# When the places of a token list are written out: list scatters paced behind an expert's products

## The chip, the cores and the metric

The kernel runs on one core of a Trainium2 chip. The metric is the device time of one execution in microseconds. The profile is of one further execution, with a record of every instruction and of the transfers.

## The reference

The input is x, 4 batches of 1,024 tokens of 256 numbers, all in float32. There are two layers.

The first is cross attention. The tokens, normalised, are the queries; 77 context vectors per batch give keys and values; there are 16 heads. The result is added to x.

The second is a mixture of experts. Each token, normalised, is sent to 2 of 9 experts by a router, and what the two give is added to it, weighted. What matters here is this part:

```python
logits = jnp.einsum('bsh,he->bse', x, Wr)
probs = jax.nn.softmax(logits, axis=-1)
topk_w, topk_idx = jax.lax.top_k(probs, TOP_K)
topk_w = topk_w / jnp.sum(topk_w, axis=-1, keepdims=True)
...
gate = jax.nn.silu(jnp.einsum('th,ehi->tei', xf, Wg))
hidden = gate * jnp.einsum('th,ehi->tei', xf, Wu)
out = jnp.einsum('tei,eih,te->th', hidden, Wd, cw)
```

An expert has two matrices of 256 x 704 (Wg, Wu) and one of 704 x 256 (Wd). The kernel computes an expert only for the tokens that chose it, so it has to make a list of tokens for each expert first.

## The kernel before

**Groups and their lists.** The 4,096 tokens are worked on in 8 groups of 512 (g = 0 to 7), each as 4 tiles of 128. The attention stage runs over the 32 tiles. For each tile TensorE makes scores (L273), ScalarE exponentials (L288), VectorE divides and turns the weights (an, anT). The turned weights go to memory and come back in another order (a_d, then aT, both on SP's queue), and TensorE multiplies them by the values (L349). Behind a group's last tile comes its routing: `choices(g)` finds the two experts of each token, `ranks(g)` counts with two small products the places in the experts' lists, and `places(g)` turns these into addresses (the tile r_pli). A list entry is a token's number and its weight (r_entry). The lists are one array in the chip's memory, list_d.

**Scatters.** `scatter()` sends one indirect transfer from GpSimd's queue (L990). It writes 128 entries of 8 bytes to 128 places of list_d. A group has 2 x 4 = 8 of them, 64 in all. `places` puts them into a queue in the program, `pending`, and for all groups but one also calls `scatter()` at once, so that they stand in GpSimd's queue right behind that point. The exception is g = NG - 3 = 5, the sixth group: its eight are left in `pending` and taken out later in `hidden_pair`, with a wait on a VectorE product (argument `behind`).

**Blocks.** The experts' work is cut into blocks: pairs (2 x 128 tokens of one expert, `hidden_pair`), ones (128 tokens, `hidden_one`), and flexible ones. Blocks 0 to 5 (EARLY = 6) are pairs that are filled from the first four groups alone (G_EARLY = 4), so that they can start before the last groups are routed. Block 0 runs together with the end of the attention stage. Each block j needs, in this order:

- the token numbers: `tokens(j)`, a gather from list_d to ids (GpSimd, L1234). For j = 0 and for j = 6 it waits until all scatters sent so far have landed;
- the tokens: `inputs(j)`, two gathers of 128 rows from y_d to yin (GpSimd, L1234, one for a block of 128), which need the ids;
- the tokens turned: for early blocks by TensorE (`turn(j)`, L1277) and ScalarE (xT); for later blocks by VectorE (`turning(j)`, L1264);
- the weights, on SP's queue (wgu and wd);
- the products: for a pair and each f from 0 to 5, up to four products of 128 x 256 (pg, L1291), a silu on ScalarE (sl, L1297) and a product on VectorE (hid, L1298);
- the second matrix: `down(j)` (L1371), scaled on VectorE to co (L1374);
- the output: `adding(j)`, indirect transfers with add from GpSimd (L1406).

**The order around the change.** The order on each engine is written out in the program; there is no planner. For block j the loop at L1605 does this: `fetch()` sends what is due ahead (the gathers of the tokens of block j + 2, the token numbers of block j + 4, the weights of block j + 2), then the products of block j, then the turn of block j + 1, then `down(j - 1)` and `adding(j - 1)`. Token numbers of block 6 and later are due only when the tables for the late blocks exist. In between, `pump()` is called behind each f. It runs pieces of the routing of the last two groups and of the late blocks' tables, up to 12 VectorE operations at a time. The routing of group 6 ends with its places in block 1, that of group 7 with its places in block 2. In block 1 the line behind the product, with `len(pending)`, sends all that is left of group 5; the eight of group 6 are sent in block 1 too, and those of group 7 in block 2, at once by `places`.

GpSimd's queue is in order: a gather or an output stands behind every scatter that was put ahead of it. The tiles yin, of which there are three, are used in turn by the blocks; so are three tiles each of r_entry and r_pli by the groups.

Of the kernel before, what the change touches and what calls it, by code (L numbers as in the profile page):

```python
# [21 lines left out]
def kernel(  # L22
# [25 lines left out]
    E, _, FF = wg.shape  # L48
# [5 lines left out]
    NG = TOK // TB  # L54
# [33 lines left out]
    G_EARLY = NG - 4  # L88
    EARLY = 6
# [38 lines left out]
    def mm_tile(name):  # L128
        return ps_mm.tile([P, TB], F32, tag="mm", name=name)
# [715 lines left out]
    def after(i, others, reason):  # L845
        for other in others:
            tc.add_manual_dep(
                i.ins, other.ins.name,
                mybir.DependencyInfo(mybir.DependencyClass.Sync, mybir.DependencyReason.DATA),
                reason=reason,  # L850
            )
# [7 lines left out]
    def small(g, name, shape=(P, NS), dt=F32, **kw):  # L859
        return pools["rpool"].tile(list(shape), dt, tag=f"r_{name}", name=f"r_{name}{g}", **kw)  # L860
# [104 lines left out]
    def places(g):  # L965

        v = nc.vector
        o, pp, entries = (routed[g][k] for k in ("o", "pp", "entries"))
        at = small(g, "at", wide)
        yield v.tensor_tensor(  # L970
            at, pp[:, : NS * E].rearrange("p (s e) -> p s e", s=NS), base, ALU.add
        )
        for k in range(2):
            yield v.tensor_tensor(o[k], o[k], at, ALU.mult)
            place, place_i = small(g, f"pl{k}"), small(g, f"pli{k}", (P, NS), I32, bufs=3)
            yield v.tensor_reduce(place, o[k], AX.X, ALU.add)
            yield v.tensor_copy(place_i, place)  # L977
            for s in range(NS):
                pending.append((place_i, entries[k], s))
                if g != NG - 3:  # L980
                    scatter()

    pending = []

    def scatter(behind=None):

        if not pending:
            return
        place_i, entry, s = pending.pop(0)
        i = nc.gpsimd.indirect_dma_start(  # L990
            out=list_d[:, :],
            out_offset=bass.IndirectOffsetOnAxis(ap=place_i[:, s : s + 1], axis=0),
            in_=entry.bitcast(I32)[:, s, :], in_offset=None,
            bounds_check=E * LP - 1, oob_is_err=False,
        )
        if behind is not None:
            after(i, [behind], "the lists' places go out one by one")

        for other in sent:
            tc.declare_no_dep(i.ins, other.ins, reason="other places of the lists")  # L1000
        sent.append(i)
# [230 lines left out]
    def gather(dst, src, offsets, bound=None):  # L1232
        kw = {} if bound is None else dict(bounds_check=bound - 1, oob_is_err=False)
        return nc.gpsimd.indirect_dma_start(  # L1234
            out=dst, out_offset=None, in_=src,
            in_offset=bass.IndirectOffsetOnAxis(ap=offsets, axis=0), **kw,
        )

    def tokens(j):

        nh, i, kind = blocks[j]
        got = gather(
            ids[j].rearrange("p h t -> p (h t)"), lists[nh], tabs[kind][1][:, i : i + 1]
        )
        if j in (0, EARLY):
            after(got, sent, "all places of the lists")
# [37 lines left out]
    def hidden_pair(j, also={}, upcoming=iter(())):  # L1284

        (w,), xT, hid = wgus.pop(j), xTs.pop(j), hids[j % 2]
        for f in range(NF + 1):
            pg = mm_tile(f"pg{j}_{f}").rearrange("p (g t) -> p g t", g=2)
            for g, at in enumerate((f * P, UP[f]) if f < NF else (f * P,)):
                for c in range(C):  # L1290
                    nc.tensor.matmul(  # L1291
                        pg[:, g, :], w[:, c, at : at + P], xT[:, c, :],
                        start=(c == 0), stop=(c == C - 1),
                    )
            sl = pools["spool"].tile([P, TS], F32, tag="sl", name=f"sl{j}_{f}")
            if f < NF:
                nc.scalar.activation(sl, pg[:, 0, :], AF.Silu)  # L1297
                made = nc.vector.tensor_tensor(hid[:, f, :], pg[:, 1, :], sl, ALU.mult)  # L1298
                for _ in range(0 if not j and f < 4 else 2 if not j else len(pending)):
                    scatter(made)  # L1300
            else:
                nc.scalar.activation(sl[64:128, :], pg[0:64, 0, :], AF.Silu)
                nc.vector.tensor_tensor(
                    hid[64:128, NF, :], pg[64:128, 0, :], sl[64:128, :], ALU.mult
                )
            pump()
            if f > 1:
                advance(upcoming, 4)
            for fn in also.get(f, ()):
                fn()  # L1310
# [109 lines left out]
    def pump():  # L1420

        if held[0]:
            held[0] -= 1
            return
        for _ in range(STEP if rest else 0):
            got = next(rest[0], None)
            if got is None:
                rest.pop(0)
                if not rest:
                    fetch()  # L1430
                return
            if got is PRODUCT:
                held[0] = HOLD
                return
# [3 lines left out]
    def fetch(in_parts=False):  # L1438

        end = NBLK if late_ready() else EARLY  # L1440
        for name, fn, lead in (
            ("weights", weights, LEAD), ("weights_upper", weights_upper, LEAD + 1),
            ("inputs", inputs, LEAD), ("tokens", tokens, LEAD + 2),
        ):
            if name == "inputs":

                while ahead["tokens"] < min(now[0] + LEAD + 1, end):
                    tokens(ahead["tokens"])
                    ahead["tokens"] += 1
            while ahead[name] < min(now[0] + lead + 1, end):  # L1450
                fn(ahead[name], in_parts) if name == "weights" else fn(ahead[name])
                ahead[name] += 1
# [8 lines left out]
    def advance(what, n=None):  # L1461

        for _ in range(n) if n is not None else iter(int, 1):
            if next(what, None) is None:
                return True
        return False
# [11 lines left out]
    def listed(g):  # L1478
        yield PRODUCT
        ranks(g)  # L1480
        yield from places(g)
# [4 lines left out]
    for i in range(N_SUB + 1):  # L1486
        g, s = divmod(i, NS)
# [57 lines left out]
        if gr >= 0 and sr == 1:  # L1545
            if g + 2 < NG:
                query_variance(g + 2)
            if q >= 0:
                advance(residual(q))
                root(q)  # L1550
            if g + 2 < NG:
                query_root(g + 2)
            nc.scalar.activation(junk, eps_t, AF.Exp)
            if q > 0:
                advance(places(q - 1))
# [49 lines left out]
    for j in range(LAST):  # L1605
# [9 lines left out]
        if j == RARE_AT - 1:  # L1615
            tokens(NBLK)
            inputs(NBLK)
# [5 lines left out]
        if blocks[j][0] == 2:  # L1623
            hidden_pair(j, {} if j else in_first, upcoming)
        else:
            hidden_one(j, upcoming)
# [22 lines left out]
    assert not rare  # L1649

    hidden_pair(LAST, {1: [lambda: down(LAST - 1), lambda: adding(*rounds_of(LAST - 1)[0])]})
    down(LAST)
    adding(*rounds_of(LAST)[0])
# [33 lines left out]
```

## Time and profile before

| | |
|---|---|
| median of three runs | 885.0 us (884.68 to 886.63) |
| the profiled execution | 887.22 us |
| its span, first to last instruction | 885.2 us |
| granted TensorE clock | 0.996 |
| TensorE busy | 98% |
| VectorE busy | 67% |
| ScalarE busy | 40% |
| GpSimd busy | 35% |
| list scatters, L990 | 64, of 1,028 ns in the mean, from 163.8 to 422.1 us |
| token gathers, L1234 (yin) | 67, of 1,060 ns in the mean |
| output transfers, L1406 (out_dram from co, ids) | 63, of 1,601 ns in the mean |

The lines of a timeline read so: start in us from the span's start, duration in us, engine, line of the kernel, operation, what it writes <- what it reads, how often; in brackets the idle time of the engine before it and what ended that time. PE is TensorE, DVE VectorE, ACT ScalarE, POOL GpSimd. A POOL row of DMA_INDIRECT is the time in which GpSimd writes the transfer's descriptors; the transfer itself lands later. In the list of waits, the numbers are us in total, how often, and the longest in us. "DMA yin<-y_d,ids" means that the engine waited for this transfer to land. The windows of TensorE's work in the stretch that is spoken of:

| us | work of TensorE |
|---|---|
| up to 352.5 | attention, tile by tile (L273, L349) |
| 352.5 to 371.6 | block 0's products, with the last attention tiles |
| 371.6 to 387.5 | block 1, then `down(0)` |
| 387.5 to 403.2 | block 2, then `down(1)` |
| 403.2 to 420.6 | block 3, then `down(2)` |
| 420.6 to 437.1 | block 4, then `down(3)` |
| 437.1 to 452.2 | block 5, then `down(4)` |

### The profile page before, as it was taken

The numbers are of one execution on the slowest core, as the hardware profiler recorded it, in microseconds if no ns is written. First come the engines' busy times: TensorE is split into PE (matmuls) and PEld (weight loads), VectorE is DVE, ScalarE is ACT, GpSimd is POOL, SyncE is SP. The second block draws the span as 40 slices with busy tenths as digits, with TensorE's granted clock in tenths as the row PEclk, the third lists the DMA queues.
The fourth block names the chain that finished last, engine by engine and source line by source line (L and its number), as shares of the span: only waits on it lengthen the run. The fifth ranks groups of instructions, "written<-read, shape, count | busy, mean of one in ns | idle before, by whom it ended". The sixth has DMA issues, their size and how long they took to land. (4 is left out here: it accounts for less than half of the span.)

```text
span 885.2 us, 13820 instructions
## 1 busy us (share of the span) xinstructions
PE 863.1 (98%) x3864; PEld 676.0 (76%) x3864; DVE 590.8 (67%) x1806; ACT 356.4 (40%) x1500; POOL 313.0 (35%) x325
## 2 busy tenths in 40 slices
PE   7999999999999999999999999999999999999996
PEld 6645787787878778987887777777777777778885
DVE  4857688998989988456445666666666666664641
ACT  3668787978879686241111111111111111111110
POOL 3000000404314350147665435435435444454332
PEclk9999999999999999999999999999999999999999
DMA  6117556667676696978788889769779777779722
GB/s 226 50 56 216 147 169 198 167 210 184 173 203 171 179 243 210 307 239 188 172 241 238 233 260 290 229 213 330 217 223 308 227 224 217 219 230 322 211 24 24
DMA packets 132956, 181.20 MB, mean 205 GB/s; under 512 B 26951, under 2 KB 98127, under 8 KB 132752
## 3 DMA queue, kind: packets, MB, share of 16 engines
q1 hardware_dynamic: 115322, 162.90, 60.2%
q0 software_dynamic: 17344, 17.29, 10.3%
q8 instruction: 31, 0.51, 0.2%
q14 instruction: 45, 0.37, 0.1%
q10 hardware_dynamic: 214, 0.13, 0.0%
HBM read 141.54 MB, written 40.41 MB: 206 GB/s over the span
## 5 line engine op out<-in xcount | busy, mean ns | idle before, releaser
L1291 PE MATMUL pg<-xT,wgu 128*128 128x256 f32 x1144 | 252.7, 379 | 1.6 <-DVEq L1640 1.5
L1291 PEld LDWEIGHTS pg<-xT,wgu 128*128 128x128 f32 x1144 | 215.7, 190 | 31.0 <-issue 1.9
L288 ACT ACTIVATE ex<-psc,mx 128x77 f32<-128x77 f32 x512 | 158.8, 331 | 59.1 <-DVE mx L277 58.9
L1371 PE MATMUL po<-wd,hid 128*128 128x256 f32 (+1 forms) x804 | 180.8, 380 | 0.0
L1371 PEld LDWEIGHTS po<-wd,hid 128*128 128x128 f32 (+1 forms) x804 | 149.2, 187 | 28.0 <-issue 3.7
L990 POOL DMA_INDIRECT list_d<-r_entry,r_pli x64 | 65.8, 1028 | 262.6 <-DVE r_pli L977 136.5
L349 PE MATMUL po<-u,aT 128*128 128x265 f32 x640 | 155.5, 398 | 1.2 <-DMA aT<-a_d 1.2
L1264 DVE STREAM_TRANSPOSE xT<-yin 32x128 f32<-32x128 f32 (+1 forms) x544 | 148.3, 273 | 11.4 <-DMA yin<-y_d,ids 3.2
L1406 POOL DMA_INDIRECT out_dram<-co,ids x63 | 100.8, 1601 | 152.0 <-DVE co L1374 127.9
L349 PEld LDWEIGHTS po<-u,aT 128*128 128x128 f32 x640 | 148.6, 312 | 1.4 <-issue 1.4
L273 PE MATMUL psc<-g,zT 128*128 128x462 f32 (+1 forms) x384 | 140.9, 513 | 1.6 <-ACT zT L262 1.5
L1297 ACT ACTIVATE sl<-pg 128x256 f32<-128x256 f32 x130 | 49.8, 384 | 226.6 <-PE pg L1291 203.0
L1298 DVE TENSOR_TENSOR hid<-pg,sl 128x256 f32<-128x256 f32 x130 | 55.0, 424 | 126.2 <-ACT sl L1297 125.5
L273 PEld LDWEIGHTS psc<-g,zT 128*128 128x128 f32 x384 | 72.1, 190 | 59.0 <-issue 45.8
L288 ACT ACTIVATION_READ_ACCUMULATOR ex<-psc,mx 128x1 f32 x512 | 108.2, 211 | 0.0
L329 DVE STREAM_TRANSPOSE anT<-an 128x1280 f32<-128x1280 f32 x32 | 79.6, 2487 | 2.4 <-DMA a_d<-anT 2.3
L1234 POOL DMA_INDIRECT yin<-y_d,ids x67 | 71.0, 1060 | 24.7 <-issue 18.9
L277 DVE TENSOR_REDUCE mx<-psc 128x6 f32<-128x462 f32 (+1 forms) x96 | 53.4, 556 | 23.2 <-PE psc L273 23.2
L1374 DVE TENSOR_SCALAR co<-po,ids 128x256 f32<-128x256 f32 x67 | 32.2, 483 | 52.6 <-PE po L1371 51.0
L310 DVE TENSOR_TENSOR an<-ex,rs 128x1024 f32<-128x1024 f32 x32 | 39.2, 1225 | 1.1
L1359 ACT COPY hid<-ph 128x384 f32<-128x384 f32 x15 | 7.2, 479 | 78.4 <-PE ph L1354 78.4
L1335 ACT ACTIVATE hs<-psg 128x512 f32<-128x512 f32 x15 | 9.0, 597 | 65.3 <-PE psg L1331 65.3
(311 smaller groups left out, 762.8 us busy)
## 6 DMA issues: line engine op xcount, KB each, us to landing
wgu<-in_L_ffn_Wg_dram SPq DMA_DIRECT2D x41, 704.0 KB
wd<-in_L_ffn_Wd_dram SPq DMA_DIRECT2D x41, 640.0 KB
wgu<-in_L_ffn_Wu_dram SPq DMA_DIRECT2D x41, 512.0 KB
a_d<-anT SPq DMA_DIRECT2D x32, 640.0 KB
aT<-a_d SPq DMA_DIRECT2D x128, 160.0 KB
wgu<-in_L_ffn_Wu_dram SPq DMA_DIRECT2D x41, 128.0 KB
x<-in_x_dram SPq DMA_DIRECT2D x8, 512.0 KB
out_dram<-x SPq DMA_DIRECT2D x8, 512.0 KB
```

The source lines that it names most:

```text
L273: nc.tensor.matmul(psc[:, :w], zT[:, c, :], g_sb[i // NS // GPB][:, c, h * J : h * J + w], start=(c == 0), stop=(c == C - 1),)
L277: nc.vector.tensor_reduce(nmx[i][:, h : h + n], psc[:, : n * J].rearrange("p (h j) -> p h j", h=n), AX.X, ALU.max, negate=True,)
L288: nc.scalar.activation(exs[i][:, h + q, :], pscs[k][:, q * J : (q + 1) * J], AF.Exp, bias=nmx[i][:, h + q : h + q + 1], accum_out=sms[i][: ...
L329: nc.vector.transpose(turned.rearrange("p q t k -> p q k t"), an_of[0].rearrange("p (k q t) -> p q k t", q=NQ, t=Q))
L349: nc.tensor.matmul(po[:, :DE], aT[:, :, n], u_sb[b][:, n, :], start=(n == 0), stop=(n == KC - 1))
L990: i = nc.gpsimd.indirect_dma_start(out=list_d[:, :], out_offset=bass.IndirectOffsetOnAxis(ap=place_i[:, s : s + 1], axis=0), in_=entry.bit ...
L1234: return nc.gpsimd.indirect_dma_start(out=dst, out_offset=None, in_=src, in_offset=bass.IndirectOffsetOnAxis(ap=offsets, axis=0), **kw,)
L1264: yield nc.vector.transpose(xT[q : q + Q].rearrange("p c (h t) -> p h c t", t=P)[:, :nh, :, a : a + Q], of(yins, j)[a : a + Q].rearrange(" ...
L1291: nc.tensor.matmul(pg[:, g, :], w[:, c, at : at + P], xT[:, c, :], start=(c == 0), stop=(c == C - 1),)
L1298: made = nc.vector.tensor_tensor(hid[:, f, :], pg[:, 1, :], sl, ALU.mult)
L1371: nc.tensor.matmul(po[rows, :D], hid[:, f, at], d[:, f, :], start=(f == 0), stop=(f == NF))
L1406: i = nc.gpsimd.indirect_dma_start(out=out_r, out_offset=bass.IndirectOffsetOnAxis(ap=rows_of(j, h, rows), axis=0), in_=cos[j][:, h, :], i ...
```

## The change

Three places of the program are edited.

1. `places`: the scatters of groups 0 to 3 are sent at once, as before. Those of groups 4, 5, 6 and 7 are now all left in `pending`.
2. `hidden_pair`: behind the VectorE product of each f from 0 to 4, scatters are taken from `pending`, each with a wait on that product. In block 0 it is none behind f = 0 and up to four behind each of f = 1 to 4; in block 1 none; in later blocks up to two behind each product.
3. `tokens`: ahead of the token numbers of block 6, what is left in `pending` is sent.

With this the queue of GpSimd holds, in block 0, the 16 scatters of groups 4 and 5; in block 2, the eight of group 6 and two of group 7; in block 3, behind f = 0, 1 and 2, the other six. None is left for block 4 or for the third edit.

```diff
             for s in range(NS):
                 pending.append((place_i, entries[k], s))
-                if g != NG - 3:
+                if g < G_EARLY:
                     scatter()
...
         nh, i, kind = blocks[j]
+        while j == EARLY and pending:
+            scatter()
         got = gather(
             ids[j].rearrange("p h t -> p (h t)"), lists[nh], tabs[kind][1][:, i : i + 1]
         )
...
                 made = nc.vector.tensor_tensor(hid[:, f, :], pg[:, 1, :], sl, ALU.mult)
-                for _ in range(0 if not j and f < 4 else 2 if not j else len(pending)):
+                for _ in range((0, 4)[f > 0] if not j else 2 if j > 1 else 0):
                     scatter(made)
```

`pending`, `scatter` and `after`, which the wait is made with, are as they were.

## The prediction

> **What bounds the kernel now.** I read first the page's busy times and the list of TensorE's waits, then TensorE's timeline at each of its stops, last GpSimd's timeline, since GpSimd's queue is what the edit rearranges.
>
> ```profile
> PE 863.1 (98%) x3864; PEld 676.0 (76%) x3864; DVE 590.8 (67%) x1806; ACT 356.4 (40%) x1500; POOL 313.0 (35%) x325
> ...
> PE px L1277 <- DMA yin<-y_d,ids: 2.8, 3, 1.8
> PE po L349 <- DMA aT<-a_d: 1.2, 1, 1.2
> ```
>
> TensorE is the bound: 98% busy at a granted clock of 0.996. So the edit can only win time where TensorE stands still. Of its stops between 300 and 450 us just these two kinds are listed, 4.0 us together; past 450 us the next gap is one of 1.5 us at 812 us, at a branch that the edit doesn't touch. Here are the four stops in the timeline:
>
> ```profile
> 333.33 4.93 PE L349 MATMUL po<-u,aT 128*128 128x265 f32 x20 [1.18 <-DMA aT<-a_d]
> ...
> 414.85 0.74 PE L1277 MATMUL px<-ident,yin 128*128 128x128 f32 x4 [1.77 <-DMA yin<-y_d,ids]
> ...
> 430.66 0.30 PE L1277 MATMUL px<-ident,yin 128*128 128x128 f32 x1 [0.39 <-DMA yin<-y_d,ids]
> 431.56 0.55 PE L1277 MATMUL px<-ident,yin 128*128 128x128 f32 x3 [0.60 <-DMA yin<-y_d,ids]
> ```
>
> The stops at 414.85 and 430.66 are the turns of the tokens of blocks 4 and 5. Why these come late stands in GpSimd's timeline:
>
> ```profile
> 371.66 1.07 POOL L990 DMA_INDIRECT list_d<-r_entry,r_pli  x1 [45.08 <-DVE hid L1298]
> ...
> 386.80 1.02 POOL L990 DMA_INDIRECT list_d<-r_entry,r_pli  x1 [5.45 <-DVE r_both L934]
> ...
> 403.51 0.98 POOL L990 DMA_INDIRECT list_d<-r_entry,r_pli  x1 [0.30 <-issue]
> ...
> 405.95 1.62 POOL L1406 DMA_INDIRECT out_dram<-co,ids  x1 [0.80 <-DMA wgu<-in_L_ffn_Wu_dram]
> ...
> 410.30 1.08 POOL L1234 DMA_INDIRECT yin<-y_d,ids  x1 [0.30 <-DVE pair_sum L1025]
> ...
> 427.13 1.08 POOL L1234 DMA_INDIRECT yin<-y_d,ids  x1 [0.30 <-issue]
> ...
> 434.19 1.02 POOL L1234 DMA_INDIRECT ids<-list_d,pair_ai  x1 [0.30 <-issue]
> ...
> 439.76 1.04 POOL L1234 DMA_INDIRECT yin<-y_d,ids  x1 [4.56 <-PE pg L1291]
> ```
>
> GpSimd is idle for 45 us, then sends 14 scatters in one run from 386.80 (1.285 us from start to start). Block 0's output, ready on VectorE from 389.25 (co, L1374), waits behind them to 405.95, and block 4's token gather to 410.30. It lands at 414.7, TensorE wanted it at 413.1. Eight more scatters at 413 to 423 hold block 5's gather to 427.13 in the same way; it is wanted at 429.9.
>
> **The change, part by part.** The counts stay: 64 scatters, the same gathers and outputs, no instruction more on TensorE, VectorE or ScalarE. What moves is the order in GpSimd's queue, and each position follows from the program text.
>
> (1) Group 4's eight scatters leave 310.46 to 320.5. The gather for block 2 that stood behind them (321.64 and 323.60) can run at about 303.5, once its token numbers have landed (303.1 in the trace's DMA records). This matters at 333.33: the weights aT of that product land at 332.4 after 5.4 us of transfer (512 packets of 1,280 bytes), where the next two aT take 3.5 and 3.4 us. The gather's 64 packets of 4,096 bytes, 269 ns each, lie at 325.7 to 331.1, inside it: 64 x 0.269 / 16 engines = 1.08 us. By bytes, 0.26 MB at about 330 GB/s, it is 0.8. From landing to the product took 0.9 us, and TensorE was ready at 332.15. So of the 1.18 I take 0.9 away; the ends are 0 (other transfers fill the place) and 1.18. At 303.5 the gather meets the aT landing at 307.5, used at 313.8: cover of over 5 us, so nothing there. The scatters themselves are 16 packets of 64 bytes at 14 to 19 ns and cost the transfers nothing, here and in block 0, where the DMA engines are full (share 0.89 to 1.05 from 352 to 387).
>
> (2) Block 0 now issues 16 scatters, four behind each of the products f=1 to 4 (361.2, 363.6, 364.6, 371.0 in the old trace). The first waits where GpSimd was idle anyway, with only group 6's token numbers and later scatters close behind. 16 x 1.285 = 20.6 from 360.6, plus 0.7 for the copies between: GpSimd is through at about 382. Block 3's gather comes next, 382 instead of 374.34, landing by about 389 (6.6 us as before); it is wanted at 397.6, so the cover is 8.6 less the 0.9 gained, 7.7. The token numbers of block 5 wait for the last scatter to land, about 387, and hold up block 0's output, which isn't ready until 388.3.
>
> (3) Block 1 issues none, so that output goes at about 389.5 and block 4's gather at 393.5 instead of 410.30. It lands near 400, wanted at 412: the 1.77 us go, with 12 us to spare.
>
> (4) Block 2 issues ten (about 396 to 409), then block 1's output to 412.7 and block 5's gather at 413 instead of 427.13, landing by 420. TensorE, now 2.7 us ahead, wants it at 427: the 0.99 us go, with 7 to spare.
>
> (5) The last six go in block 3 behind f=0 to 2. VectorE is late there with the late blocks' tables (its f=2 product ran at 411.18, 2 us behind ScalarE), so they run from 416 to 423.3. Block 2's output follows to 427. Block 6's token numbers need all scatters landed: 422 + 6.6 to 8.0 (landings at that load) = 430, instead of 434.19. They land 4.8 later, and block 6's gather goes at 435.6, its data in by 439.5. Before it was 439.76, with the last packet at 443.6 and TensorE at 446.62. TensorE will be there at 442.9: cover 3.4, before 3.0. This is the tightest place. From there GpSimd is about 4 to 5 us earlier than before and TensorE 3.7, so nothing later loses cover.
>
> The waits on products hold GpSimd alone. Behind its tile reuse nothing is late: VectorE's entries of group 7 reuse group 4's tile, whose scatters have landed by about 376 and are needed landed at 388.
>
> Here the Trainium skill speaks against the change. "SBUF — State Buffer", in "SBUF: two separate sides", says that GpSimd can't write descriptors while a VectorE copy holds the port pair that they share, and that a GpSimd transfer of 620 ns took 3,100 beside one. Pacing scatters behind VectorE's work invites that. The row: 64 scatters of 972/980/1644 ns (least, median, most), and the run of 14 beside VectorE's products and group 7's small operations has none over 1.02 us. By the row the pacing costs nothing. By the page, 16 x 2.5 = 40 us more in block 0 would bring block 3's gather to 422, and TensorE would stop for 40 - 7.7 = 32 us at 397: a sum of 885.2 - 3.7 + 32 = 914. I take the row, 881.5.
>
> A second rule sizes the chain of (5). "DMA: Bandwidth & Descriptors", "Anatomy of one DMA — SWDGE (gpsimd) path", gives about 2 us for a small transfer. The trace's scatters land after 2.8/4.7/8.1. By the page the cover at block 6 would be 11 us instead of 3.4; I keep the row.
>
> Sum: 0.9 + 1.77 + 0.99 = 3.66. The profiled execution has a span of 885.2 and 887.22 in all; its span should become 881.5. The median of the three timed runs, 885.0, lies within 0.2 of that span, and I take the same 3.7 off: 881.3. Each us that TensorE starts earlier should reach the end, as the tail (8.2 us of outputs behind the last product) is unchanged.
>
> **The rivals.** Partly: the stop at 333 stays, because the output and weight transfers queued there fill the gap, or half of block 5's stays. Then 2.76 or 2.3 are saved: 882.2 to 882.7. For it: DMA share 0.91 from 310 to 333.5 without any help from GpSimd. Against: the 5.4 beside 3.5 us. Chance 0.15.
>
> Given back: the landings in (5) take 8 us three times over instead of 8, 4.8 and 4, so block 6's gather is in at about 446.5, and 3.6 is lost there again: about 884.9, no change. For it: old landings up to 8.9 at 447. Against: scatters and block 2's output are over by 427, and the DMA share of 0.81 from 420 to 437 is 0.60 behind that. Chance 0.10.
>
> Slower: the port lock. Its place is the scatters of blocks 0 and 2, beside VectorE's small copies. What a scatter takes over 1.285 us from start to start counts 16-fold ahead of block 3's gather. With the cover of 7.7 block 3 is late from 1.77 us on, and from 2.0 us on more is lost than the 3.7 gained. At 2.2 the time is about 888, at the page's price 914. For it: four of the earlier scatters took 1.50 to 1.64. Against: no more than one in a run of eight did, and the others took about 0.98. Chance 0.06.
>
> That the order doesn't change can't be: the positions are fixed in the program.
>
> **How the numbers follow.** All three gains 0.69, at 881.3, own range 880.5 to 882.0; partly 0.15; given back 0.10; slower 0.06. A measurement of this kernel tells 0.2% (1.8 us) from no change: the three runs spread over 1.95. Faster is the first two less 0.02, for a mixture in which only one stop goes: 0.82. Those 0.02 and most of the third make same 0.11; the rest, with the fourth, makes slower 0.07. The range leaves out the lower tail of the first case and everything slower than a nearly full give-back: 880.2 to 883.8.
>
> **What would show it.** Right: no stop of TensorE before L1279 (the turn's new line) at blocks 4 and 5; the stop before L349 at 332 under 0.4 us; GpSimd's first wait on a product at 361 instead of 371; block 0's output at about 390. Wrong: a stop of TensorE at block 3 (397) or at block 6 (443), scatters over 1.6 us in block 0, or aT later than 332.4.

## The result, and the profile after

The changed kernel took 890.8 us (median of 13 runs, 888.43 to 894.43) against 887.87 us for the kernel before beside it (13 runs, 884.68 to 889.48): a ratio of 1.004, interval 1.0026 to 1.0055. It is slower, by 0.4%; 881.3 with a range up to 883.8 was forecast. Ratios and intervals, here and below, are taken over the fast runs and aren't quotients of the medians shown. The profiled execution took 891.61 us, span 889.6, clock 0.995; the span of before was 885.2.

The page and TensorE's list of waits from 300 to 460 us, changed kernel (us in total, times, longest):

```profile
PE 864.9 (97%) x3864; PEld 676.9 (76%) x3864; DVE 591.2 (66%) x1806; ACT 356.4 (40%) x1500; POOL 312.1 (35%) x325
...
PE px L1279 <- DMA yin<-y_d,ids: 5.9, 3, 2.8
PE psc L273 <- ACT zT L262: 0.4, 1, 0.4
```

The stop before L349 is gone from the list, a wait of 0.42 us for ScalarE at 300 us is new, and the waits for token gathers have grown from 2.8 to 5.9 us. TensorE's timeline shows where:

```profile
332.39 4.86 PE L349 MATMUL po<-u,aT 128*128 128x265 f32 x20
...
412.21 0.60 PE L1279 MATMUL px<-ident,yin 128*128 128x128 f32 x4
...
428.67 0.64 PE L1279 MATMUL px<-ident,yin 128*128 128x128 f32 x4 [1.18 <-DMA yin<-y_d,ids]
429.14 5.35 PE L1373 MATMUL po<-wd,hid 128*128 128x256 f32 x24
...
445.82 0.30 PE L1279 MATMUL px<-ident,yin 128*128 128x128 f32 x1 [1.84 <-DMA yin<-y_d,ids]
448.96 0.90 PE L1279 MATMUL px<-ident,yin 128*128 128x128 f32 x3 [2.83 <-DMA yin<-y_d,ids]
449.65 7.13 PE L1373 MATMUL po<-wd,hid 128*128 128x256 f32 x24
```

The stops at 333 and at block 4's turn are gone, block 5's is still there (1.18), and block 6's turn, where before had none, stands for 1.84 + 2.83 = 4.67 us. Behind it the same 24 products of `down` take 7.13 us instead of 5.35. TensorE's windows there say why (length, busy time and count, granted clock, DMA share, GB/s):

```profile
core 0: us, PE busy (x), PEclk, DMA share, GB/s
...
444.00:446.44 2.44, 0.30 (x1) 1.00 0.60 162
446.44:453.27 6.83, 4.31 (x12) 0.50 0.91 235
453.27:466.00 12.73, 12.73 (x61) 1.00 0.73 208
```

The clock is halved for 6.83 us. TensorE worked 4.31 us of these, so that costs about 2.15 (half of the work, an estimate). Without its stops and this the changed kernel would have 889.6 - 1.18 - 4.67 - 2.15 = 881.6; the kernel before without its four stops has 885.2 - 3.94 = 881.3. So stops and clock account for the difference within 0.3 us. Of the forecast gain of 3.66 us, 2.95 is there (the stop at 333 and block 4's turn); block 5's 0.99 isn't, and what is lost on top is at block 6's turn.

GpSimd's timeline tells why these gathers are late:

```profile
360.89 1.03 POOL L990 DMA_INDIRECT list_d<-r_entry,r_pli  x1 [53.56 <-DVE r_top L931]
...
381.37 0.98 POOL L990 DMA_INDIRECT list_d<-r_entry,r_pli  x1 [0.31 <-issue]
382.66 1.05 POOL L1234 DMA_INDIRECT yin<-y_d,ids  x1 [0.31 <-issue]
...
394.67 0.98 POOL L1234 DMA_INDIRECT ids<-list_d,early_ai  x1 [9.63 <-DMA list_d<-r_entry,r_pli]
...
397.13 1.65 POOL L1408 DMA_INDIRECT out_dram<-co,ids  x1 [0.81 <-DMA wgu<-in_L_ffn_Wu_dram]
...
400.94 1.08 POOL L1234 DMA_INDIRECT yin<-y_d,ids  x1 [0.30 <-issue]
...
420.60 1.07 POOL L1234 DMA_INDIRECT yin<-y_d,ids  x1 [0.30 <-issue]
...
429.79 0.98 POOL L990 DMA_INDIRECT list_d<-r_entry,r_pli  x1 [0.30 <-DMA list_d<-r_entry,r_pli]
...
438.79 1.02 POOL L1234 DMA_INDIRECT ids<-list_d,pair_ai  x1 [4.26 <-DMA list_d<-r_entry,r_pli]
442.83 1.04 POOL L1234 DMA_INDIRECT yin<-y_d,ids  x1 [3.03 <-issue]
```

The 16 scatters of block 0 go as forecast, 360.89 to 381.37. Then the read of block 5's token numbers (394.67) waits 9.63 us, until the last of them has landed at 393.92: 12.55 us after its issue. From there GpSimd has no pause until 434.5. Block 0's output goes at 397.13 instead of 389.5, and everything behind it is 7 to 9 us later than forecast: block 4's gather, block 5's, the last scatter, block 6's token numbers, block 6's gather.

### The profile page after: what moved, and what is told of

Its sections match the earlier page's. It is cut to its first block, busy times and chain, and to the rows that moved or that the text cites. A ratio compares the mean times of both kernels' runs of the same rounds, so it can differ in the third digit from the quotient of the medians.

```text
span 889.6 us, 13823 instructions
## 1 busy us (share of the span) xinstructions
PE 864.9 (97%) x3864; PEld 676.9 (76%) x3864; DVE 591.2 (66%) x1806; ACT 356.4 (40%) x1500; POOL 312.1 (35%) x325
## 5 line engine op out<-in xcount | busy, mean ns | idle before, releaser
L1293 PE MATMUL pg<-xT,wgu 128*128 128x256 f32 x1144 | 252.7, 379 | 1.6 <-DVEq L1642 1.5
L1293 PEld LDWEIGHTS pg<-xT,wgu 128*128 128x128 f32 x1144 | 215.7, 190 | 31.0 <-issue 1.9
L1373 PE MATMUL po<-wd,hid 128*128 128x256 f32 (+1 forms) x804 | 182.6, 382 | 0.0
L1373 PEld LDWEIGHTS po<-wd,hid 128*128 128x128 f32 (+1 forms) x804 | 150.5, 189 | 28.5 <-issue 3.7
L349 PE MATMUL po<-u,aT 128*128 128x265 f32 x640 | 155.4, 398 | 0.0
L349 PEld LDWEIGHTS po<-u,aT 128*128 128x128 f32 x640 | 148.7, 312 | 0.1
```

Source lines behind the costliest of these rows:

```text
L349: nc.tensor.matmul(po[:, :DE], aT[:, :, n], u_sb[b][:, n, :], start=(n == 0), stop=(n == KC - 1))
L1293: nc.tensor.matmul(pg[:, g, :], w[:, c, at : at + P], xT[:, c, :], start=(c == 0), stop=(c == C - 1),)
L1373: nc.tensor.matmul(po[rows, :D], hid[:, f, at], d[:, f, :], start=(f == 0), stop=(f == NF))
```

## The experiments

Two theories at first. The *landing theory*: the wait for the landings of block 0's scatters, in front of block 5's token numbers, makes GpSimd late. The *pace theory*: the waits behind products in blocks 2 and 3 spread the scatters too far, whatever happens in block 0. There were five batches, each on one chip, each with the kernel before beside it:

| batch | before, us | what ran |
|---|---|---|
| 1 | 899.88 (67 runs) | e1 to e4 |
| 2 | 885.85 (62) | e5 to e8 |
| 3 | 887.35 (25) | e9 to e12 |
| 4 | 888.19 (23) | e13 to e16 |
| 5 | 887.26 (17) | e17, e18 |

**Batch 1: four parts of the change.** e1 reads block 5's token numbers ahead of block 0's scatters:

```diff
-            ("inputs", inputs, LEAD), ("tokens", tokens, LEAD + 2),
+            ("inputs", inputs, LEAD), ("tokens", tokens, LEAD + 2 + (now[0] == 0)),
```

e2 sends group 4's scatters at once again (`if g < G_EARLY + 1`), so that block 0 has eight; e3 those of groups 6 and 7 (`if g < G_EARLY or g > NG - 3`). e4 asks for block 3's weights one block later, so that they aren't transferred under block 0's scatters:

```diff
-            ("weights", weights, LEAD), ("weights_upper", weights_upper, LEAD + 1),
+            ("weights", weights, LEAD - (now[0] == 1)), ("weights_upper", weights_upper, LEAD + 1),
```

> The changed kernel with one gather moved: the token numbers of block 5 are read before block 0's sixteen scatters, so that GpSimd no longer waits, between blocks 0 and 1, until the last of these has landed (10.7 us from the gather at 384.0 to 394.67 in the changed kernel). Landing theory (the scatters land late while the DMA engines are full, 12.6 us for the last instead of the 6.6 that I reckoned with, and this one wait hands that to everything behind it): block 0's output goes at about 389 instead of 397.1, blocks 5 and 6 get their tokens 7 us earlier, the stops of 1.18 and 4.67 us are gone, and with them the halved clock behind the second: span about 882, ratio to the kernel before 0.995 to 0.998. Pace theory (two scatters behind each product reach into block 3 whatever comes before, and block 6's list is complete too late): the stop at block 6 stays over 3 us, ratio 1.002 to 1.005.

> The changed kernel with group 4's eight scatters sent at once, as in the kernel before; blocks 0, 2 and 3 keep the fixed pace. Block 0 then sends eight scatters, not sixteen. Landing theory: the last of them is sent at about 372 and landed by 380, the token numbers of block 5 go at about 380, block 0's output at 389; no stop at blocks 5 and 6, but the stop of about 1.2 us at 333 (weights of the attention behind block 2's gather) is back: span about 883, ratio 0.996 to 0.999. Pace theory: as the changed kernel, a stop over 3 us at block 6, ratio 1.002 to 1.005.

> The other half alone: groups 4 and 5 go behind block 0's products as in the changed kernel, groups 6 and 7 are sent at once in blocks 1 and 2, as in the kernel before. Landing theory: the token numbers of block 5 go at 394.7 as in the changed kernel, then group 6's eight scatters, block 0's output at 406, block 4's tokens asked for at 410 and landed by 416, wanted at 412: a stop of 3 to 5 us at block 4 with a halved clock behind it; none at block 6, whose list is complete earlier. Span 888 to 891, ratio 1.002 to 1.006. Pace theory: the late pace was the cause and is gone, so this one is as fast as the kernel before or faster, 0.996 to 1.000.

> The changed kernel, with the order of GpSimd's queue untouched, but the weights of block 3 (2.1 MB) asked for one block later, so that these transfers are not among those that fill the DMA engines from 371 to 387. Landing theory: the last scatter of block 0 lands within about 8 us instead of 12.6, block 5's token numbers go at about 389 instead of 394.7, and the stops at blocks 5 and 6 shrink from 5.9 us together to under 1.5: span 882 to 885, ratio 0.996 to 1.000. If the DMA load has nothing to do with the late landings, nothing changes: ratio 1.002 to 1.005, last landing still over 11 us.

Measured: 900.6 (ratio 1.000, 0.9978 to 1.0022), 896.63 (0.9969, 0.9951 to 0.9988), 896.93 (0.9968, 0.995 to 0.9986), 900.24 (1.0009, 0.9987 to 1.0031). By the ratios e2 lies in the landing theory's range, e3 in the pace theory's, and e1 and e4 in neither. This chip ran the kernels some 11 to 18 us longer, the one before by 12 to 14, and in these traces TensorE stood before the products of `hidden_pair` and `down` (L1293, L1373), as in none of the others, and nowhere for a gather. So I take no verdict on the theories from them; why this chip differs is open. One reading remains: with the weights moved away (e4), block 5's token numbers went at 384.43 after a wait of 0.58 us, in e3, with the same scatters ahead, at 390.87 after 5.73.

**Batch 2: both kernels unedited, and the two edits again.**

> The kernel before, unedited, for its trace on the chip of this batch. Both theories: ratio 1.000 within the noise; stops before the turns of blocks 4 and 5 and before the attention product at 333, as in its first trace. If the stops lie elsewhere (at products that wait for ScalarE or VectorE, as in the four traces of the last batch), this chip shows a disturbance of its own, and ratios from it say little about either theory.

> The changed kernel, unedited, beside it. Both theories: ratio 1.002 to 1.006, stops at blocks 5 and 6, the token numbers of block 5 held back behind the last scatter of block 0.

> The changed kernel with the token numbers of block 5 read before block 0's scatters, again, now beside traces of both kernels on the same chip. Landing theory: faster than the changed kernel by 0.4 to 0.9%, no stop at blocks 5 and 6. Pace theory: as the changed kernel.

> The changed kernel with group 4 sent at once, again. Landing theory: faster than the changed kernel by 0.3 to 0.8%, a stop of about 1.2 us at 333, none at blocks 5 and 6. Pace theory: as the changed kernel.

| | median us (range) | ratio to before, interval | token numbers of 5 | block 0's output | block 6's second gather | stops at block 6 |
|---|---|---|---|---|---|---|
| e5, before | 884.28 (883.3 to 886.03) | 0.9983, 0.9969 to 0.9998 | 379.83 | 404.83 | 438.90 | none |
| e6, changed | 884.43 (880.73 to 889.79) | 0.9988, 0.9974 to 1.0003 | 391.35 | 393.81 | 440.61 | 0.88 |
| e7, numbers first | 882.55 (880.38 to 884.38) | 0.9966, 0.9954 to 0.9977 | early | 389.34 | 433.94 | none |
| e8, group 4 at once | 882.17 (880.15 to 885.24) | 0.9962, 0.9951 to 0.9973 | 378.96 | 387.82 | 432.76 | none |

On this chip the changed kernel equals the one before, which neither theory had given. e5 and its partner are one program, and yet its interval leaves out 1: differences of about 0.2% don't separate two kernels here. e7 and e8 are 0.2 and 0.3% under e6, less than the landing theory gave. But they keep the pace of blocks 2 and 3 and have no stop between 300 and 800 us but one of 0.19 (e8, before L349): the pace theory falls. The landing theory stands so far.

**Batch 3: the weights again, and the same edit in the kernel before.** e9 is the changed kernel, e10 is e4's edit, e11 is the kernel *before* with e1's edit, e12 has the edits of e7 and e8 together.

> The changed kernel unedited, as the partner of the other three. Landing theory: its time hangs on when the last scatter of block 0 lands. If block 5's token numbers go by 391.5, as on the quiet chip, it stands within 0.15% of the kernel before; if they go at 394 or later, as in the first profile, TensorE stops at block 6's turn for over 2 us and the ratio is 1.002 to 1.006. Pace theory: a stop behind the products of blocks 2 and 3 in every run, 0.3% to 0.5% above before.

> The weights of block 3 are asked for one block later, so that they are no longer transferred under block 0's scatters; the scatters are as in the changed kernel. If the transfers of weights are what holds the landings up: the last scatter lands within 5 us, block 5's token numbers go by 386, no stop at the turns of blocks 4 to 6, and the time is that of the two edits that took the wait away (ratio about 0.9965), unless block 3's weights now come late at 396 (a stop there of up to 2 us, ratio up to 0.999). If the number of scatters in flight holds them up: the token numbers still go at 390 or later and the time is that of the changed kernel beside it.

> The kernel before with the one edit that helped the changed kernel: block 5's token numbers are read one block earlier. Landing theory: before has two scatters ahead of these token numbers in block 0, and its stops at the turns of blocks 4 and 5 come from the 14 scatters in one run, which stay; so within 0.15% of before. If that edit helps by itself, whatever the pace: ratio 0.9965, as with the changed kernel.

> The changed kernel with both edits: the fifth group's scatters go at once, and block 5's token numbers are read one block earlier. Landing theory: each edit alone already takes every stop between 300 and 800 us away, so together they bring no more: ratio to before 0.996 to 0.997, no stop. If the two act on different losses: 0.994.

Measured: e9 890.89 (880.82 to 894.5; 1.0008, 0.9979 to 1.0037; the quotient of the medians would be 1.004), e10 882.33 (0.9935, 0.9912 to 0.9958), e11 883.09 (0.994, 0.9917 to 0.9963), e12 884.01 (0.9958, 0.9942 to 0.9975). e12 is as expected, no more than either edit alone, but for a stop of 0.97 us at 333. e10 has no stop, but the last scatter still took 7.57 us to land and the token numbers went at 389.43, not by 386: its gain can't come from that wait alone. And e11 contradicts the theory as I had put it: the edit helps before as much. Its GpSimd timeline:

```profile
375.44 1.04 POOL L1234 DMA_INDIRECT yin<-y_d,ids  x1 [0.30 <-issue]
376.79 1.02 POOL L990 DMA_INDIRECT list_d<-r_entry,r_pli  x1 [0.31 <-DVE mv_f L879]
...
396.43 1.62 POOL L1406 DMA_INDIRECT out_dram<-co,ids  x1 [0.80 <-DVE hid L1298]
```

The run of 14 scatters starts at 376.79, not at 386.80. What held it in before was the read of block 5's token numbers from the list. (The program text asks for a wait for all scatters at blocks 0 and 6 alone; in the traces this read waits for those ahead of it too.) It waited for two scatters to land and went at 380.38; it landed at 386.04, and the next scatter, which writes the list that it reads, went 0.76 us later (in e5: 384.88, and 0.76 later). The profile had put that wait down to `r_both` on VectorE (L934), which in e5 runs only after the scatter has gone. So a read between scatters costs two landings.

**Batch 4: that read moved the other way, and the clock.** e16 is the kernel before with the read one block later (`LEAD + 2 - (now[0] == 1)`): behind the 14 scatters and block 4's gather. e15 is e7's kernel again; e13 and e14 add to it one or two more issues of block 6's gather, each waiting for the landing of the one before (n = 2, 3):

```diff
-            gather(of(yins, j)[:, h, :], y_d[:bound, :], ids[j][:, h, 0:1], bound)
+            for _ in range(1 + (n - 1) * (j == EARLY)):
+                gather(of(yins, j)[:, h, :], y_d[:bound, :], ids[j][:, h, 0:1], bound)
```

> The changed kernel with block 5's token numbers read first (no stop between 300 and 800 us), and block 6's token gather issued twice, each issue waiting for the landing of the one before: some 3.6 us later for each of its two halves. Its cover was 3.2 us, so TensorE should stop 2 to 4 us at block 6's turn. If a stop halves the clock: one spell of 3.41 us at half clock (or 6.8), so the time grows by the stop and 1.7 to 3.4 more. If the dip had another cause: by the stop alone, clock as in the partner.

> The same with block 6's gather issued three times: 14 us later than in the partner, a stop of 9 to 11 us at block 6's turn. If a stop halves the clock: 6.8 us or more at half clock behind it, so 12 to 15 us over the partner. If not: 9 to 11 us over it. Block 7's gather comes 14 us later as well, but TensorE does too by 10 or more, so at most a short stop there.

> The partner of the two before: the changed kernel with block 5's token numbers read before block 0's scatters, as on the second chip. Ratio to before 0.994 to 0.998, no stop between 300 and 800 us, no spell at half clock there.

> The kernel before with block 5's token numbers read one block later: behind the run of 14 scatters and block 4's gather, ahead of group 7's eight. If the read is what held the run back (it waits for the scatters ahead of it to land, and the scatters behind it wait until it has landed): the 14 start at about 377 instead of 386, block 0's output goes at 396 and block 4's gather at 400, no stop at block 4's turn; the read then goes at about 403, the eight at 409, and block 5's gather at 423, landing at 429, just in time or up to 1 us late: ratio 0.996 to 1.000. If the run of 14 by itself delays block 4's gather, or the routing's work on VectorE held it: the stop at block 4's turn stays, ratio 0.999 to 1.002.

e16: 886.44 (0.9988, 0.9969 to 1.0007), within what the read's theory gave. Its places came 1.4 to 2.4 us before those written down:

```profile
374.64 1.02 POOL L990 DMA_INDIRECT list_d<-r_entry,r_pli  x1 [0.31 <-DVE mv_f L879]
...
398.28 1.07 POOL L1234 DMA_INDIRECT yin<-y_d,ids  x1 [0.31 <-PE po L1371]
...
400.99 0.97 POOL L1234 DMA_INDIRECT ids<-list_d,early_ai  x1 [0.31 <-issue]
407.27 1.01 POOL L990 DMA_INDIRECT list_d<-r_entry,r_pli  x1 [5.32 <-DVE pair_sum L1025]
```

Block 4's stop is gone, block 5's is 1.04, and the price of the read has moved to 407.27: 5.32 us of waiting for its landing.

e15 missed: 889.52 (1.0002, 0.9978 to 1.0026), with stops of 4.87 and 1.19 at block 6's turn, though nothing waits for the scatters. GpSimd's timeline of e15:

```profile
386.20 0.31 POOL L951 COPY r_entry<-r_tg 128x4 int32<-128x4 int32 x2
396.28 1.65 POOL L1408 DMA_INDIRECT out_dram<-co,ids  x1 [9.77 <-DVE hid L1300]
```

The output still waits until 396.28, while VectorE, which the profile names, had made the first half at 389.24. Block 0's output adds to rows of `out_dram`, so x of the last group must have been written there first (L870, on SP's queue at 380.97). In the trace's semaphore records this write lands at 395.29. GpSimd's own wait for that semaphore, of the output's line, lasts from 386.34 to 395.32 (in e7 from 385.13 to 388.38), and the output goes 0.99 us after the landing. In e14 it is 395.12 and 0.99, in e13 391.23 and 0.99, in e7 388.36 and 0.98. So block 0's output goes at the latest of three moments: 2.46 us behind the read, which is the time of the read itself and the two small operations behind it in the queue; 0.99 us behind x's landing; or 0.28 us behind the first half of co. The three constants are read from these traces. With them it holds within 0.02 us in all ten traces of the paced order (batch 1 and the repeated gathers left out; e17 belongs to the last batch):

| | read of 5's numbers + 2.46 | x landed + 0.99 | first half of co + 0.28 | output | block 6's second gather | stops at block 6 |
|---|---|---|---|---|---|---|
| first profile | 394.67: 397.13 | 394.12: 395.11 | 388.72: 389.00 | 397.13 | 444.18 | 4.67 |
| e18, changed | 392.68: 395.14 | 392.63: 393.62 | 387.94: 388.22 | 395.14 | 442.61 | 5.92 |
| e6, changed | 391.35: 393.81 | 389.52: 390.51 | 388.53: 388.81 | 393.81 | 440.61 | 0.88 |
| e9, changed | 390.65: 393.11 | 390.23: 391.22 | 386.72: 387.00 | 393.11 | 439.55 | 2.65 |
| e15 | early | 395.29: 396.28 | 389.24: 389.52 | 396.28 | 443.74 | 6.06 |
| e7 | early | 388.36: 389.35 | 388.51: 388.79 | 389.34 | 433.94 | none |
| e12 | early | 388.73: 389.72 | 389.44: 389.72 | 389.72 | 436.85 | none |
| e8 | 378.96: 381.42 | 385.34: 386.33 | 387.54: 387.82 | 387.82 | 432.76 | none |
| e10 | 389.43: 391.89 | 381.69: 382.68 | 388.49: 388.77 | 391.87 | 438.20 | none |
| e17 | early | 381.85: 382.84 | 386.67: 386.95 | 386.95 | 434.11 | none |

From the output to block 6's second gather it is 44.6 to 47.5 us in each of them: but for waits ahead of block 6 (4.26 and 3.03 us in the first profile) the queue between is full, and one late start goes through to the end. It also fits e10, whose edit takes x's write forward by 10 us (asked for at 368.8 instead of 378.9) and so removes one wait and shortens the other.

e13 and e14: 893.04 (1.0068, 1.0041 to 1.0094) and 902.5 us (1.015, 1.0124 to 1.0177), with stops of 9.14 and 16.23 us at block 6's turn; the expectation had counted from e7, but beside them e15 itself stood 6.06. Half clock: 6.83 us in e15, 10.24 in e13, 17.07 in e14. TensorE's windows in e14:

```profile
core 0: us, PE busy (x), PEclk, DMA share, GB/s
...
443.80:447.56 3.76, 0.04 (x1) 1.00 0.69 228
447.56:464.63 17.07, 4.56 (x13) 0.50 0.33 86
464.63:475.00 10.37, 10.37 (x50) 1.00 0.74 194
```

The spell grows with the stop, its price hardly: in it TensorE works 3.36, 3.80 and 4.56 us, so about 1.7, 1.9 and 2.3 us are lost. What I had expected (3.4 us and more) took the spell's length for its price. e14's median is 13.0 us over e15's, within the 12 to 15 expected, but longer stops and price make only 10.8 of it; the rest is open. No trace of batches 2 to 5 with less than 2.6 us of stops at one turn has such a spell between 300 and 800 us.

**Batch 5: both waits away.** e17 is the changed kernel with the edits of e1 and e4; e18 is the changed kernel.

> The changed kernel with both edits: block 5's token numbers read before block 0's scatters, and block 3's weights asked for one block later, so that x's write no longer queues behind them. If these two landings are the whole cause: x's last packet by 385, block 0's output at 387 to 391, as soon as VectorE has made it, the token numbers of block 6 at 426 to 430, no stop of TensorE between 300 and 800 us and no half clock there, whatever the chip's transfers do: ratio 0.992 to 0.996. If something else holds GpSimd's queue (the scatters' own pace, the late blocks' tables): stops at block 6's turn stay on a chip where the changed kernel has them, ratio 0.998 or more.

> The changed kernel unedited, beside e17. Its output goes at the later of two moments, 2.5 us behind the read of block 5's token numbers or within 1 us of x's last packet; if that is 394 or later, it has stops of over 2 us at block 6's turn and a spell at half clock, ratio 1.001 to 1.006; if it is 391 or earlier, ratio 0.997 to 1.000.

e17: 882.17 us (880.66 to 882.94), ratio 0.9943, 0.9923 to 0.9963. e18: 889.38 (883.58 to 894.56), 1.0027, 1.0004 to 1.005. Both came as expected. GpSimd in e17:

```profile
386.95 1.65 POOL L1408 DMA_INDIRECT out_dram<-co,ids  x1 [3.48 <-DMA wgu<-in_L_ffn_Wu_dram]
...
425.79 1.02 POOL L1234 DMA_INDIRECT ids<-list_d,pair_ai  x1 [1.37 <-issue]
432.76 1.04 POOL L1234 DMA_INDIRECT yin<-y_d,ids  x1 [5.95 <-PE pg L1293]
```

The output goes when VectorE has made it, block 6's gather 10 us earlier than in the first profile, and there is no stop and no half clock from 300 to 800 us: span 878.6. On the same chip the two edits are worth 7.2 us. e10, e11, e12 and e17 beat both kernels beside them by 0.4 to 1.0%; their intervals overlap, so none of them is shown to be the best. e7 and e8 are 0.2 to 0.3% under both unedited kernels of their batch, and e7's order, as e15, gained nothing on another chip. e10, with the weights alone moved, does as well as e17, though its read still waits 4.63 us: there that wait by itself cost TensorE nothing.

## Why the prediction was wrong

- **(1) was right.** The product at 332.39 waits for nothing. With group 4's scatters put back the stop returns: 0.97 us at 333.03 in e12, though just 0.19 in e8, on a chip where the kernel before has 0.46 (e5).
- **(2) failed, at its last sentence.** The scatters went where it said. "The token numbers of block 5 wait for the last scatter to land, about 387": it landed at 393.92, since landings of 6.3 us at the head of the run grew to 12.55 at its end, where the sum took the 6.6 of a stretch with two scatters. "Hold up block 0's output, which isn't ready until 388.3": ready it was at 388.72, but besides the read it waits for x's write, which the step didn't name; landed at 386.34 before and at 394.12 after, it would alone have held the output to 395.11. Of the 7.6 us (397.13 - 389.5) the read's wait alone makes 2.0; 5.6 are doubly held. That is why e15, with the read moved, gained nothing on its chip.
- **"The scatters themselves cost the transfers nothing"** doesn't fit the traces, and probably lies under both. Windows of the kernel before, then of the changed one:

```profile
core 0: us, PE busy (x) PEld busy (x) DVE busy (x) ACT busy (x) POOL busy (x), PEclk, DMA share, GB/s
360.00:385.00 25.00, 25.00 (x122) 22.46 (x121) 10.90 (x53) 10.65 (x20) 5.13 (x5) 1.00 1.04 346
```

```profile
360.00:385.00 25.00, 25.00 (x122) 22.46 (x121) 10.88 (x55) 10.42 (x20) 18.37 (x21) 1.00 1.01 268
```

  The DMA engines are as busy (share 1.04 and 1.01), but move 268 GB/s instead of 346; GpSimd has 18.37 us of work there instead of 5.13. In the trace's DMA records SP's queue moves 8.35 MB in these 25 us before and 6.65 after, 5 us' worth, and its packets of 2,816 bytes take 190 ns instead of 139. With the same weights asked for, by the packets of 64 bytes in that stretch: 32 to 80 of them, 8.11 to 8.35 MB; 96 to 128, 7.48 to 7.76; 216 to 241, 6.57 to 7.71 (14 traces). Chips differ as much: one order moved 7.55 MB in e7 and 6.74 in e15. On each chip that has both, the kernels with 216 or more lie below those with 32 to 128, on that of batch 2 by little (7.71 against 7.76 in e8, 8.23 in e5). A scatter's own packet shows 15 ns. No run changed the scatters' number or size and nothing else, so the cause is argued, not shown.
- **(3) and (4).** Block 4's gather went at 400.94 instead of 393.5; with 12 us to spare its stop of 1.77 is gone, as forecast. Block 5's went at 420.60 instead of 413, 7.6 late, and landed at 428.71, after 8.1 instead of 7: the 7 to spare weren't enough.
- **(5)** rightly named the tightest place. Its chain is as long as it said, 37.4 us from block 0's output to the end of block 2's, then 4.3 for the last landing, where the sum had 3; it only began 7.6 late. With cover of 3.4 TensorE stood 4.67.
- **The clock** wasn't in the sum: 2.15 us more behind that stop. The Trainium skill, "TensorE: Matmul & The Clock Gate", "Part 1: The HAM clock gate", has it: after about 3.4 us without work the clock is halved, and comes back after as long at work. The spells here are 3.41, 6.83, 10.24 and 17.07 us, one, two, three and five times that; but stops of 2.65 us, in two parts, were enough (e9).
- **The rivals.** "Slower" by the port lock is refuted here: no scatter of block 0 took over 1.03 us. "Given back" had the right place, block 6's gather, but not the right landings: those of (5) took 8.2, 3.3 and 4.7 us, nearly the sum's 8, 4.8 and 4, and the long ones were block 0's. In "Partly" half of block 5's stop left by itself would save 3.2 us; the 2.3 is both together.

So the step that failed is (2): a landing taken as 387 was 394, and beside it stood a wait, for x's write, that had been left out. The mechanism of the gain was right at two of its three places, 2.95 us in the trace. How large the loss is goes with how late the two landings are: the same kernel stands at 0.9988, 1.0008, 1.0027 and 1.004 of before in four comparisons. Over its 59 timed runs there the time follows the granted clock: median 884.2 us at 0.996 and above (21 runs), 892.0 at 0.991 and below (14). A spell of 6.83 us at half clock lowers the mean by just 0.004, and the profiled run stands at 0.995: runs at 0.991 and below hold more half clock than its trace shows, and they have no trace.

## What to carry to other kernels

A read of a buffer that scatters write is a double barrier in an in-order queue: it waits until all scatters ahead have landed, and those behind wait until it has. Put it ahead of the first or far behind the last, and list for each instruction behind it *every* transfer that it needs landed, with its time in the new order. A landing time taken where few transfers are in flight isn't good for a place where the edit itself puts sixteen.

## What the runs showed that I had not expected

- With more scatters of 64-byte packets in flight the large packets beside them took longer: 346 to 268 GB/s, with the engines no less busy. Whether the scatters do it, and why, is open.
- A transfer has landed when the last of 16 parts has: x's write reported its parts from 388.70 to 394.12. The Trainium skill, "DMA: Bandwidth & Descriptors", "Why a DMA increments its semaphore by 16 and not by 1", says that only the full sixteen count; here the slowest part made 5.4 us.
- The half-clock spell follows stops well under 3.4 us. In the 3.41 us ahead of it TensorE stood for 1.95 us in e9 and for 2.16 in the first profile; before's stop of 1.77 us brought none.
- What makes one chip's transfers slower than another's (x's write landed at 388.36 in e7, at 395.29 in e15, the same program) stays open.
